# Area attention in a two-layer vision network: where the fill-in projections stand, half sums ahead of the means, and every odd exponential summed by DMA

## The chip, the cores and the metric

The kernel runs on one core of a Trainium2 chip. The metric is the device time of one execution in microseconds (us); three runs before the change took 2905.74, 2909.25 and 2912.93 us, the median being 2909.25 us.

A core has engines that run side by side, each with its own queue of instructions in program order: TensorE (PE in the profile, with its weight loads as PEld), VectorE (DVE), ScalarE (ACT), GpSimd (POOL) and SyncE (SP, which only issues transfers here). An instruction starts when the ones before it in its own queue have started and the semaphores it names have been raised by others. Sixteen DMA engines move data; a DMA that adds into its destination is issued from POOL's queue here.

## The reference, cut to what matters

The network has four parts (attention, a recurrent layer, convolutions with a state-space scan, experts). Only the first one changes:

```python
def _ln_c(v, eps=1e-6):                       # over the 256 channels
    m = jnp.mean(v, axis=1, keepdims=True)
    s = jnp.var(v, axis=1, keepdims=True)
    return (v - m) / jnp.sqrt(s + eps)

x = x + _L0_conv_ref(_ln_c(x), ...)           # x: (2, 256, 64, 64)

# inside _L0_conv_ref: 8 heads of 32 channels, areas of 1024 pixels (16 rows)
qk = _conv1x1_bn(x, w_qk, ...);  vv = _conv1x1_bn(x, w_v, ...)
pp = _bn(conv 5x5, depthwise, of vv)
attn = softmax(einsum('bhdn,bhdm->bhnm', q, k) * hd ** -0.5)
o = einsum('bhdm,bhnm->bhdn', v, attn)
return _conv1x1_bn(o + pp, w_proj, ...)
```

Everything is float32. There are 2 images of 4 areas each, so 8 areas of 1024 tokens, and in each area 8 heads.

## The kernel before

`area_attention` holds the image in SBUF as two channel halves of 128 partitions (`x[:, c]`). An area has two *groups*, one for each channel half `c` (four heads each), so there are 16 groups; `G` numbers the groups and `A` the areas. A group is 16 *steps*: `t = 8 n + m`, where `n` is the half of the queries (512 columns) and `m` a block of 128 keys. The loop over `g` from 0 to 255 writes out the order of all queues by hand; nothing is moved by a scheduler.

One step issues, in this order:

- `scores` (L366 to L385): four bfloat16 matmuls L371 (each row's maximum, in three parts, from `mxs`) and four float32 matmuls L376 into two PSUM tiles of two banks (`wide`, three buffers); ACT takes the exponentials of both, L383, into `sx` (for `m % 4 == 0`) or `ex` (two buffers of each).
- `values` of the step before (L389 into `av_o`).
- `maxima` of the *next* group (L276, again two `wide` tiles): in even steps ACT keeps their positive part (L288), in odd steps DVE finishes them with four reductions (L292). Four tiles a step pass through three buffers, so the second half of the next step's scores needs the buffer of this step's first maxima tile.
- the sums of the softmax, in fours: `total` is the `sx` pair of `m % 4 == 0`; half 0 of every later exponential is added to it by an accumulating DMA from POOL's queue (L591); half 1 by a POOL addition in odd `m` (L593, held back by a hand-made dependency until the DVE reductions begin) and by a DVE addition where `m % 4 == 2` (L600). Two steps after its last addition, `sums` multiplies the total with ones on PE (L389 into `po`), and at every second call DVE turns, inverts and multiplies (L415 to L423).
- taps: 50 DVE operations an area (L335, L346) for the 5x5 convolution, as many a step as the table `TAPS` says.
- the fill-in work of other areas from the tables `MINE`, `SMALL`, `LATE`, `AROUND`, `LATE_AROUND` (with `_FIRST` variants for group 0): projections `query`, `key`, `v_half`, `output` (L166, four passes on PE for 512 columns), `v_tokens` (transposes L239), `mean` and `variance` (L178: both channel halves times a constant matrix), `place` (L316 and small transfers). All of it shares one PSUM bank, `po`. The entries named "around" hold offsets in areas, the others in groups.

An area's norm runs through these steps of the even group (`c = 0`) for the next area: `centre` (DVE L187), `square` (ACT L190), `variance` (PE L178, ACT L179), `root` (DVE transpose L199, POOL L202 and L203, DVE L206), `scale` (DVE L212). `mean` of the area after that stands in the odd group.

The last group has no maxima to prepare, and the one before it no projections of a next area. After the last step, DVE adds the taps and PE projects the last area (L621).

Of the kernel before, what the change touches and what calls it, by code (L numbers as in the profile page):

```python
# [14 lines left out]
ALU = mybir.AluOpType  # L15
# [78 lines left out]
def area_attention(tc, sh, ap):  # L94
# [13 lines left out]
    with ExitStack() as ctx:  # L108
# [30 lines left out]

        minus_half = cp.tile([P, 1], F32, name="minus_half")  # L140
        nc.gpsimd.memset(minus_half, -0.5)
        latest = [None]

        def mark(op):

            latest[0] = op.ins

        def wide():
            return ps1.tile([P, 2, 512], F32, name="ps", tag="ps")

# [19 lines left out]
        def area(A):  # L170
            b, a = AREAS[A]
            return x[:, :, b, a * NA : (a + 1) * NA]

        def average(src, to, half):

            ps = bank()
            for c in range(2):
                nc.tensor.matmul(ps, sh.mean_w, src[c][:, HALVES[half]], start=c == 0, stop=c == 1)  # L178
            nc.scalar.copy(to[:, HALVES[half]], ps)  # L179

        def mean(A, half):
            average([area(A)[:, c] for c in range(2)], temp("pm", A), half)

        def centre(A, c, at=FULL):
            if A not in xns:
                xns[A] = p1.tile([P, 2, NA], F32, name="xn")
            mark(nc.vector.tensor_tensor(xns[A][:, c, at], area(A)[:, c, at], temp("pm", A)[:, at], ALU.subtract))  # L187

        def square(A, c, at=FULL):
            nc.scalar.activation(temp(f"sq{c}", A)[:, at], xns[A][:, c, at], AF.Square)  # L190
# [4 lines left out]
        def root(A, part, at=FULL):  # L195
            n = (at.stop - at.start) // 32
            if part == 0:
                turned = temp("ln_t", A)[:, at]
                mark(nc.vector.transpose(turned, temp("var", A)[:, at]))  # L199
                t = turned.rearrange("p (k i) -> p k i", i=32)[:, :, 0]  # L200
                y = held["root", at.start] = p1.tile([P, NA // 32], F32, name="root")[:, :n]
                nc.gpsimd.tensor_scalar(y, t, 1e-6, None, ALU.add)  # L202
                nc.gpsimd.tensor_tensor(y, y, minus_half.to_broadcast([P, n]), ALU.pow)  # L203
            else:
                y = held.pop(("root", at.start))
                mark(nc.vector.transpose(  # L206
                    temp("ln_r", A)[:, at].rearrange("p (k i) -> p k i", i=32),
                    y.unsqueeze(2).to_broadcast([P, n, 32]),
                ))

        def scale(A, c, at=FULL):
            mark(nc.vector.tensor_tensor(xns[A][:, c, at], xns[A][:, c, at], temp("ln_r", A)[:, at], ALU.mult))  # L212

        def columns(t):
            return lambda k: t[:, k]
# [112 lines left out]
        def taps(A):  # L328

            vh, a = vhs[A], AREAS[A][1]  # L330
            for lower in range(2):
                for c in range(2):
                    if not lower:
                        acc = accs[A, c] = p1.tile([P, AROWS, WW], F32, name=f"acc{c}")
                        nc.vector.tensor_scalar(  # L335
                            acc, vh[:, c, 2 : 2 + AROWS], w_pe[:, c, 12:13], t_pe[:, c : c + 1], ALU.mult, ALU.add
                        )
                        yield
                    for k in range(25):
                        dy, dx = k // 5 - 2, k % 5 - 2  # L340
                        if dy == 0 and dx == 0 or (dy > 0) != lower:
                            continue
                        r0, r1 = window(dy, AROWS, AROWS * a, HH)
                        w0, w1 = window(dx, WW)
                        part = accs[A, c][:, r0:r1, w0:w1]
                        mark(nc.vector.scalar_tensor_tensor(  # L346
                            part, vh[:, c, 2 + r0 + dy : 2 + r1 + dy, w0 + dx : w1 + dx],
                            w_pe[:, c, k : k + 1], part, ALU.mult, ALU.add,
                        ))
                        yield  # L350

        def add_taps(A, c):
            y = ys[A, c]
            mark(nc.vector.tensor_tensor(y, y, accs.pop((A, c)).rearrange("p r w -> p (r w)"), ALU.add))

        def output(A, co, half):
            ps, to = bank(), area(A)[:, co, HALVES[half]]
            project(w["wpr"], co, lambda k: ys[A, k], half, ps)
            mark(nc.vector.scalar_tensor_tensor(to, ps, s_pr[:, co : co + 1], to, ALU.mult, ALU.add))

        def shift(A, co):

# [41 lines left out]
        def sums(G, n, half, exs):  # L404
# [15 lines left out]
            nc.vector.transpose(  # L420
                total.rearrange("p (k i) -> p k i", i=32), small.unsqueeze(2).to_broadcast([P, 512 // 32, 32])
            )
            mark(nc.vector.tensor_tensor(y, y, total, ALU.mult))  # L423

        with ExitStack() as own:
# [58 lines left out]
            maxima(0, 7)  # L486
            join(0, 0, nc.vector)
            place(0, 0)
            v_tokens(0, 0, 1)
            query(0, 1)  # L490

            w_pe = cp.tile([P, 2, 25], F32, name="w_pe")
            for c in range(2):
# [5 lines left out]

        MINE = {0: [(1, query, 1)], 11: [(2, query, 0)], 12: [(2, key, 0)], 15: [(2, key, 1)]}
        SMALL = {2: [(0, place, 1)], 10: [(1, place, 0)]}
        LATE = {7: [(1, join, 0)], 15: [(2, key_difference), (1, join, 1)]}
        AROUND = [
            {
                1: [(-1, shift, 0)], 2: [(0, v_tokens, 1, 0)], 3: [(0, v_tokens, 1, 1)], 4: [(1, variance, 0)],
                5: [(-1, shift, 1)], 6: [(1, variance, 1)], 7: [(-1, output, 0, 0)], 8: [(-1, output, 0, 1)],
                10: [(-1, output, 1, 0)], 14: [(1, v_half, 0, 0)],
            },  # L510
            {
                2: [(1, v_half, 1, 0)], 3: [(1, v_half, 0, 1)], 4: [(1, v_half, 1, 1)],
                6: [(-1, output, 1, 1)], 7: [(1, v_tokens, 0, 0)], 8: [(1, v_tokens, 0, 1)],
                10: [(2, mean, 0)], 14: [(2, mean, 1)],
            },
        ]
        LATE_AROUND = [
            {
                0: [(1, centre, 0)], 1: [(1, square, 0)], 2: [(1, centre, 1), (-1, add_taps, 1)],
                3: [(1, square, 1)], 6: [(1, root, 0)],  # L520
                8: [(1, root, 1), (1, scale, 0)], 10: [(1, scale, 1)],
            },
            {15: [(0, add_taps, 0)]},
        ]

        FIRST = {
            0: [(1, key, 1)], 1: [(1, query, 1)], 11: [(2, query, 0)], 12: [(2, key, 0)], 15: [(2, key, 1)],
        }
        SMALL_FIRST = {5: [(0, place, 1)], 10: [(1, place, 0)]}
        LATE_FIRST = {  # L530
            0: [(1, key_difference)], 3: [(0, join, 1)], 7: [(1, join, 0)], 15: [(2, key_difference), (1, join, 1)],
        }
        LATE_AROUND_FIRST = {
            1: [(1, centre, 0)], 2: [(1, centre, 1), (1, square, 0)], 3: [(1, square, 1)],
            6: [(1, root, 0)], 8: [(1, root, 1), (1, scale, 0)], 9: [(1, scale, 1)],
        }


        AHEAD = {t: [(1, t)] for t in range(16)}
# [2 lines left out]
        for t in range(16):  # L542
            AHEAD_FIRST[t] = [order.pop(0) for _ in range(2 if t < 8 else 1)]

        TAPS = [
            [1, 0, 0, 2, 2, 2, 2, 1, 0, 0, 1, 2, 2, 2, 3, 2],
            [2, 0, 2, 2, 3, 2, 2, 1, 1, 0, 3, 2, 3, 2, 2, 1],
        ]
        TAPS_FIRST = [
            [0] * 10 + [1, 2, 3, 2, 3, 2],  # L550
            [2, 0, 2, 2, 3, 3, 3, 2, 2, 0, 3, 3, 3, 3, 3, 3],
        ]

        def works(G, t, *tables):
# [7 lines left out]
                    f(at, *a)  # L562

        pending, due, total = None, {}, None
        at_end = mybir.DependencyInfo(mybir.DependencyClass.Sync, mybir.DependencyReason.DATA)
        conv = iter(())
        for g in range(16 * len(GROUPS)):
            G, t = divmod(g, 16)
# [10 lines left out]
            exs = scores(G, n, m)  # L579
            if pending is not None:  # L580
                values(*pending)
            works(G, t, SMALL_FIRST if new else SMALL, {})

            mm, before = None, latest[0]
            for k, at in (AHEAD_FIRST if new else AHEAD).get(t, ()):
                if G + k < len(GROUPS):
                    mm = maxima(G + k, at)
            if m % 4 == 0:
                total = exs
            else:  # L590
                nc.gpsimd.dma_start(total[0], exs[0], accum_op=ALU.add)  # L591
            if m % 2:
                add = nc.gpsimd.tensor_tensor(total[1], total[1], exs[1], ALU.add)  # L593
                if mm is not None:
                    tc.add_manual_dep(add.ins, mm.name, at_end, reason="beside the reductions")
                    tc.add_manual_dep(add.ins, before.name, at_end, reason="beside the reductions")
            for _ in range((TAPS_FIRST if A == 0 else TAPS)[c][t]):
                next(conv, None)
            if m % 4 == 2:
                mark(nc.vector.tensor_tensor(total[1], total[1], exs[1], ALU.add))  # L600
            works(G, t, FIRST if new else MINE, AROUND[c])
            if g in due:
                sums(*due.pop(g))
            works(G, t, LATE_FIRST if new else LATE, LATE_AROUND_FIRST if new else LATE_AROUND[c])
            pending = G, n, m, exs
            if m % 4 == 3:
                due[g + 2] = G, n, m // 4, total

        values(*pending)
        last = len(AREAS) - 1  # L610
# [1712 lines left out]
```

## Time and profile before

| what | us |
|---|---|
| median of three runs | 2909.25 |
| the profiled execution, and its span | 2907.71, 2905.9 |
| first step of group 0 starts at | 62.2 |
| groups 0 and 1 | 96.7 and 86.8 |
| groups 2 to 12, from 245.8 to 1157.4 | 82.9 each in the mean (82.2 to 84.4) |
| groups 13 and 14 | 81.5 and 76.6 |
| group 15 and the last projection, 1315.5 to 1402.6 | 87.1 |

The starts of the steps are read off the timeline of PE: a step begins with the first of the four matmuls L371. The steps repeat from group to group almost to the hundredth: in group 4 (from 412.6) they take 5.39, 4.43, 4.40, 4.61, 6.08, 4.43, 5.68, 5.40, 5.35, 4.43, 5.73, 5.40, 5.35, 4.43, 5.68 and 5.40 us. What comes after 1402.6 us (half of the span) isn't touched by the change.

### The profile page before, as it was taken

Reading aid. Unit: us, or ns where it says so; the run is one execution under the profiler, and the core shown is the slowest. Engines: PE = TensorE matmul, PEld = TensorE weight load, DVE = VectorE, ACT = ScalarE, POOL = GpSimd, SP = SyncE. Lnnn points to the kernel's source line nnn. Section 1 sums busy time; section 2 is a strip of 40 time slices with the busy share of each in tenths; the row PEclk is TensorE's granted clock in tenths of the full one; section 3 lists DMA queues with packets and bytes.
Section 4 is the critical chain, followed back from the end, with each engine's and each line's share of the span. In section 5 each row is a group of like instructions: output and inputs, shape, how many; then the busy total and the mean of one; then the engine's idle time right before and its main releaser. Section 6 shows DMA issues by size and latency. Waiting matters only on the chain.

```text
span 2905.9 us, 45896 instructions
## 1 busy us (share of the span) xinstructions
PE 2650.5 (91%) x17286; PEld 1490.6 (51%) x17286; DVE 1991.1 (69%) x3765; ACT 1562.2 (54%) x2641; POOL 1289.3 (44%) x1115
## 2 busy tenths in 40 slices
PE   7999999999999999998799999968886599999994
PEld 2223333333333333222599999933343488888873
DVE  4789888888888888879566666788897622222116
ACT  3667676676767676665244555567645522222223
POOL 1454545444554545445213000058772166666651
PEclk9999999999999999998799999989998799999995
DMA  3333443434343434445231000035552366666658
GB/s 131 66 73 74 80 81 73 81 74 81 75 79 74 80 73 81 78 79 100 80 126 65 1 1 2 1 86 150 143 149 94 113 216 232 220 229 229 221 177 348
DMA packets 86393, 321.04 MB, mean 110 GB/s; under 512 B 17608, under 2 KB 18512, under 8 KB 76432
## 3 DMA queue, kind: packets, MB, share of 16 engines
q0 software_dynamic: 53056, 225.88, 30.5%
q1 hardware_dynamic: 31872, 87.86, 9.4%
q10 hardware_dynamic: 1232, 4.25, 0.4%
q8 instruction: 139, 2.28, 0.3%
q14 instruction: 94, 0.77, 0.1%
HBM read 173.30 MB, written 43.58 MB: 75 GB/s over the span
## 4 chain that ended last, share of the span: by engine, by line
PE 74%; DVE 10%; issue 5%; DMA 4%; POOL 4%; ACT 3%; SPq 0%; DVEq 0%; POOLq 0%; ACTq 0%
PE ps L276 9%; PE ph L2069 9%; PE py L2079 8%; PE av_o L389 7%; PE z L796 7%; PE po L166 7%; PE z L808 7%; PE ps L376 6%; PE ps L371 3%; DMA sx<-ex 2%; DVE hs L1541 2%; PE yp L1551 2%; PE po L178 2%; PE po L389 2%; PE px L2057 1%
## 5 line engine op out<-in xcount | busy, mean ns | idle before, releaser
L346 DVE SCALAR_TENSOR_TENSOR acc<-vh,w_pe,acc 128x1008 f32<-128x1008 f32 (+7 forms) x384 | 534.0, 1393 | 9.5
L383 ACT ACTIVATE ex<-ps 128x1024 f32<-128x1024 f32 x384 | 372.8, 1024 | 177.2 <-PE ps L376 101.9
L591 POOL DMA_DIRECT2D sx<-ex x192 | 167.9, 875 | 594.6 <-ACT ex L383 273.5
L292 DVE CUSTOM_DVE_ANT_0 more<-ps,more 128x512 f32<-128x512 f32 x480 | 303.0, 687 | 154.6 <-PE ps L276 146.0
L2071 ACT ACTIVATE act<-ph,wt 128x256 f32<-128x256 f32 x272 | 128.8, 474 | 386.1 <-PE ph L2069 381.9
L593 POOL TENSOR_TENSOR sx<-sx,ex 128x1024 f32<-128x1024 f32 x128 | 324.5, 2535 | 12.3 <-PE ps L276 6.9
L2059 DVE COPY xt<-px 128x512 f32<-128x512 f32 x68 | 47.1, 692 | 396.7 <-PE px L2057 396.7
L2069 PE MATMUL ph<-xt,wt 128*128 128x256 f32 x1088 | 291.7, 391 | 4.7 <-ACT act L2071 3.0
L376 PE MATMUL ps<-q,k 32*128 32x512 f32 x2048 | 290.9, 607 | 0.0
L2079 PE MATMUL py<-wt,act 128*128 128x256 f32 x1088 | 278.8, 379 | 0.0
L288 ACT ACTIVATE more<-ps 128x1024 f32<-128x1024 f32 x240 | 233.1, 1025 | 30.3 <-ACT rows L320 7.8
L2069 PEld LDWEIGHTS ph<-xt,wt 128*128 128x128 f32 x1088 | 190.7, 191 | 67.0 <-DVE xt L2059 23.5
L796 PE MATMUL z<-xs,u 128*128 128x128 f32 x1872 | 224.5, 277 | 0.0
L796 PEld LDWEIGHTS z<-xs,u 128*128 128x128 f32 x1872 | 218.2, 194 | 0.2 <-issue 0.2
L2079 PEld LDWEIGHTS py<-wt,act 128*128 128x128 f32 x1088 | 202.0, 190 | 24.5
L820 ACT ACTIVATE t<-z,bias 128x128 f32<-128x128 f32 x468 | 136.3, 362 | 145.6 <-PE z L808 145.4
L389 PE MATMUL av_o<-ex,vt 128*32 128x512 f32 x1536 | 208.7, 613 | 0.2 <-ACT ex L383 0.2
L2094 POOL DMA_INDIRECT results<-y,ri x136 | 138.0, 1015 | 138.4 <-DVE y L2087 116.4
L276 PE MATMUL ps<-k,q 32*128 32x512 f32 x1088 | 186.5, 640 | 1.4 <-DVE nm L282 0.7
L808 PE MATMUL z<-xs,v 128*128 128x128 f32 x1512 | 180.1, 276 | 0.1
L808 PEld LDWEIGHTS z<-xs,v 128*128 128x128 f32 x1512 | 174.3, 192 | 0.7 <-DVE xs L827 0.7
L1548 POOL TENSOR_TENSOR cs<-hs,cs 128x1024 f32<-128x1024 f32 x63 | 148.9, 2365 | 54.4 <-DVE hs L1541 33.5
(431 smaller groups left out, 4535.8 us busy)
## 6 DMA issues: line engine op xcount, KB each, us to landing
sx<-ex POOLq DMA_DIRECT2D x192, 512.0 KB, 4.6
cs<-c_rows SPq DMA_DIRECT2D x128, 256.0 KB
y<-results SPq DMA_DIRECT2D x32, 512.0 KB
x<-xrows SPq DMA_DIRECT2D x8, 1024.0 KB
rows<-xt SPq DMA_DIRECT2D x16, 512.0 KB
out_x<-res POOLq DMA_DIRECT2D x15, 512.0 KB, 7.0
xrows<-xn SPq DMA_DIRECT2D x24, 256.0 KB
x<-in_x SPq DMA_DIRECT2D x4, 1024.0 KB
```

What stands on the lines that cost most here:

```text
L276: mm = nc.tensor.matmul(tiles[h // 2][:, h % 2], qs[G, i // HM][head(h), i % HM * P : (i % HM + 1) * P], keys[head(h)], start=True, stop=T ...
L288: nc.scalar.activation(held["more"][j], tiles[j], AF.Relu)
L292: nc.vector.tensor_tensor_reduce(more, tiles[h // 2][:, h % 2], more, -1.0, 3.0e38, ALU.add, ALU.min, accum_out=nms[G][:, 0, h, i : i + 1],)
L346: mark(nc.vector.scalar_tensor_tensor(part, vh[:, c, 2 + r0 + dy : 2 + r1 + dy, w0 + dx : w1 + dx], w_pe[:, c, k : k + 1], part, ALU.mult, ...
L376: nc.tensor.matmul(tiles[h // 2][:, h % 2], k[head(h), m % HM * P : (m % HM + 1) * P], qs[G, n][head(h)], start=False, stop=True, tile_pos ...
L383: nc.scalar.activation(exs[i], tiles[i], AF.Exp, scale=HD**-0.5)
L389: nc.tensor.matmul(to[head(h)], lhs, exs[h // 2][:, h % 2], start=first, stop=last, tile_position=(0, HD * h))
L593: add = nc.gpsimd.tensor_tensor(total[1], total[1], exs[1], ALU.add)
L796: nc.tensor.matmul(z[c][:, g, :m], u[:, k, c, g], xt[:, k], start=g == GATES[0] and k == 0, stop=False, skip_group_check=True,)
L808: nc.tensor.matmul(z[c][:, g, :m], v[:, k, c, g], h[:, k], start=False, stop=k == 1, skip_group_check=True,)
L2069: nc.tensor.matmul(ph[:, hc], wt[:, at : at + P], xt[:, c], start=c == 0, stop=c == 1)
L2079: nc.tensor.matmul(py[:, j], act[:, hc, j * P : j * P + P], wt[:, at : at + C], start=hc == 0, stop=hc == NH - 1,)
```

## The change

The step's order becomes a `BEFORE` table (ahead of the maxima), the maxima, the transfers, and then, in even steps, taps, the `BEHIND` tables, `sums`, the `LATE` tables; in odd steps `BEHIND`, `sums`, taps, `LATE`. In the tables the full projections stand in odd steps (apart from step 0 and the two halves of the variance in step 4), and the sums and most transposes in even ones. `sums` comes three steps after its total instead of two. The POOL additions go, and so do the hand-made dependencies: in odd `m`, half 1 is added by a second accumulating DMA. The DVE addition moves from `m % 4 == 2` behind the maxima to `m % 4 == 3` ahead of them. Two DVE additions an area are new (`mean_sum`, `square_sum`), and the mean and the variance multiply their result alone. One batch of transposes moves from the prologue into step 1.

```diff
-            for c in range(2):
-                nc.tensor.matmul(ps, sh.mean_w, src[c][:, HALVES[half]], start=c == 0, stop=c == 1)
+            for c in range(len(src)):
+                nc.tensor.matmul(
+                    ps, sh.mean_w, src[c][:, HALVES[half]], start=c == 0, stop=c == len(src) - 1
+                )
...
+        def mean_sum(A):
+            nc.vector.tensor_tensor(temp("pm", A), area(A)[:, 0], area(A)[:, 1], ALU.add)
+        def mean_of_sum(A, half):
+            average([temp("pm", A)], temp("pm", A), half)
+        def square_sum(A):
+            nc.vector.tensor_tensor(temp("sq0", A), temp("sq0", A), temp("sq1", A), ALU.add)
+        def variance_of_sum(A, half):
+            average([temp("sq0", A)], temp("var", A), half)
...
-            v_tokens(0, 0, 1)
             query(0, 1)
...
+        BEFORE = [
+            {0: [(1, query, 1)], 3: [(0, place, 1)], 11: [(1, place, 0)]},
+            {3: [(0, place, 1)], 11: [(1, place, 0)]},
+        ]
+        BEFORE_AREA = [{4: [(1, variance_of_sum, 0)]}, {0: [(1, v_half, 0, 0)]}]
+        BEHIND = [
+            {11: [(2, query, 0)], 13: [(2, key, 0)], 15: [(2, key, 1)]},
+            {5: [(1, query, 1)], 9: [(2, query, 0)], 13: [(2, key, 0)], 15: [(2, key, 1)]},
+        ]
+        BEHIND_AREA = [
             {
+                1: [(0, v_tokens, 0, 1), (-1, shift, 0)], 3: [(0, v_tokens, 1, 0)], 4: [(1, variance_of_sum, 1)],
+                5: [(-1, output, 0, 0), (-1, shift, 1)], 7: [(-1, output, 0, 1)], 9: [(-1, output, 1, 0)],
+                12: [(0, v_tokens, 1, 1)],
             },
             {
+                1: [(1, v_half, 1, 0)], 3: [(1, v_half, 0, 1)], 4: [(2, mean_of_sum, 0)],
+                7: [(-1, output, 1, 1)], 8: [(2, mean_of_sum, 1)], 11: [(1, v_half, 1, 1)],
+                12: [(1, v_tokens, 0, 0)],
             },
         ]
+        LATE = {7: [(1, join, 0)], 15: [(2, key_difference), (1, join, 1)]}
+        LATE_AREA = [
             {
+                0: [(1, centre, 0)], 1: [(1, centre, 1), (1, square, 0)], 2: [(1, square, 1)],
+                3: [(-1, add_taps, 1), (1, square_sum)], 5: [(1, root, 0)], 7: [(1, root, 1), (1, scale, 0)],
+                8: [(1, scale, 1)],
             },
+            {3: [(2, mean_sum)], 15: [(0, add_taps, 0)]},
         ]
...
         TAPS = [
-            [1, 0, 0, 2, 2, 2, 2, 1, 0, 0, 1, 2, 2, 2, 3, 2],
-            [2, 0, 2, 2, 3, 2, 2, 1, 1, 0, 3, 2, 3, 2, 2, 1],
+            [2, 0, 0, 1, 2, 2, 1, 1, 0, 1, 0, 3, 2, 2, 2, 3],
+            [2, 1, 1, 2, 2, 2, 2, 2, 2, 1, 1, 3, 2, 2, 2, 1],
         ]
         TAPS_FIRST = [
-            [0] * 10 + [1, 2, 3, 2, 3, 2],
-            [2, 0, 2, 2, 3, 3, 3, 2, 2, 0, 3, 3, 3, 3, 3, 3],
+            [0, 0, 0, 0, 1, 1, 1, 1, 1, 1, 2, 2, 3, 2, 3, 2],
+            [2, 1, 2, 2, 2, 2, 2, 2, 2, 1, 2, 2, 2, 2, 2, 2],
         ]
...
+            if m % 4 == 3:
+                nc.vector.tensor_tensor(total[1], total[1], pending[3][1], ALU.add)
             for k, at in (AHEAD_FIRST if new else AHEAD).get(t, ()):
...
-            else:
-                nc.gpsimd.dma_start(total[0], exs[0], accum_op=ALU.add)
-            if m % 2:
-                add = nc.gpsimd.tensor_tensor(total[1], total[1], exs[1], ALU.add)
-                if mm is not None:
-                    tc.add_manual_dep(add.ins, mm.name, at_end, reason="beside the reductions")
-                    tc.add_manual_dep(add.ins, before.name, at_end, reason="beside the reductions")
-            for _ in range((TAPS_FIRST if A == 0 else TAPS)[c][t]):
-                next(conv, None)
-            if m % 4 == 2:
-                mark(nc.vector.tensor_tensor(total[1], total[1], exs[1], ALU.add))
+            for i in ((), (0, 1), (0,), (0, 1))[m % 4]:
+                nc.gpsimd.dma_start(total[i], exs[i], accum_op=ALU.add)
...
-                due[g + 2] = G, n, m // 4, total
+                due[g + 3] = G, n, m // 4, total
```

An entry such as `4: [(1, variance_of_sum, 0)]` means: in step 4, half 0 of the variance of the next area; the first of the two tables of a pair is for even groups (`c = 0`), the second for odd ones.

## The prediction

> **What bounds the kernel now.** First the page: who is busy where.
>
> ```profile
> PE 2650.5 (91%) x17286; PEld 1490.6 (51%) x17286; DVE 1991.1 (69%) x3765; ACT 1562.2 (54%) x2641; POOL 1289.3 (44%) x1115
> ...
> PE   7999999999999999998799999968886599999994
> ...
> DVE  4789888888888888879566666788897622222116
> ```
>
> The attention is the first 19 or so of 40 slices (to 1402.6 us). There PE is at 9 and DVE at 8: PE sets the pace and DVE has little to spare. By stretches of one group each (columns: length, then busy time of PE, PEld, DVE, ACT, POOL; clock; DMA share):
>
> ```profile
> 412.60:494.80 82.20, 81.29 (x535) 25.42 (x538) 71.87 (x111) 58.68 (x67) 44.01 (x34) 1.00 0.41 78
> ...
> 1315.50:1402.60 87.10, 64.45 (x394) 16.98 (x389) 71.94 (x68) 33.87 (x38) 38.83 (x29) 0.82 0.42 79
> ```
>
> Group 4 shows PE busy for 81.3 of 82.2 us and DVE for 71.9, at full clock. The last group is different: PE is idle for 23 us. Now PE's timeline, steps 5 and 6 of group 4:
>
> ```profile
> 437.49 0.39 PE L371 MATMUL ps<-mx,ones_b 3*128 3x512 bf16 x4
> 437.71 1.03 PE L376 MATMUL ps<-q,k 32*128 32x512 f32 x8
> 438.67 1.06 PE L389 MATMUL av_o<-sx,vt 128*32 128x512 f32 x8
> 439.67 1.32 PE L276 MATMUL ps<-k,q 32*128 32x512 f32 x8
> 440.92 1.06 PE L389 MATMUL po<-sx,ones 128*32 128x512 f32 x8
> 441.92 0.79 PE L371 MATMUL ps<-mx,ones_b 3*128 3x512 bf16 x4
> 442.32 1.24 PE L376 MATMUL ps<-q,k 32*128 32x512 f32 x8
> ...
> 445.68 1.98 PE L178 MATMUL po<-sq,mean_w 128*128 128x512 f32 x4
> 447.60 0.40 PE L371 MATMUL ps<-mx,ones_b 3*128 3x512 bf16 x4
> ```
>
> Differences of starts price a step: 0.22 + 0.96 + 1.00 + 1.25 = 3.43 us bare; the sums add 1.00, a projection 1.92 (445.68 to 447.60), half of that 0.96, a batch of transposes 0.58, `place` 0.16. A step with sums is 4.43, with a projection 5.35. The step behind the sums has L371 0.79 and L376 1.24 for 0.39 and 1.03: its second half waited for a buffer, and 5.68 us passed instead of 5.35. So a short filler in an odd step isn't free: DVE's reductions (starting 0.03 after the maxima, 0.61 each) release the buffer at 3.46 + 1.22 = 4.7 us into the step.
>
> **The change in PE's queue.** A pair of groups holds 32 bare steps (109.8), 20 projections (38.4; 16 true ones and the four of mean and variance, which cost as much), 8 sums (8.0), 4 batches (2.3) and 4 places (0.6): 159.1 of 2 x 82.9 = 165.7 us. Multiplying a sum instead of two halves makes those four 0.96 each and saves 3.8 us. The rest of what could be won is the 6.6 us of waits.
>
> By step, behind the change: an odd step with a projection 5.35 (the buffer at 4.7 is early enough). An even step with sums: ACT's L288 pair starts when the maxima end, 3.45, its first takes 1.02, so the buffer comes at 4.5: 4.5 whatever the short filler. Step 8 also has the copy of `av_o` (0.59, pitch 0.5) ahead of it, so about 4.8. Steps 3 and 11 with `place` 5.5. Step 0, which took 5.4 to 7.2 us because the maxima waited for POOL's `kd`, now has a projection ahead of them: 5.35. The odd group: seven projections 37.5, two with place 11.0, five short steps 22.5, step 8 4.8, step 4 4.5: 80.3. The even group from step 5 to step 0 of the next: 6 x 5.35 + 5.5 + 4 x 4.5 + 4.8 = 60.4; its steps 1 to 4 come below.
>
> **The two new DVE additions**, 1.24 us each (row of L600, 128x1024, mean 1239 ns), lie beside PE, but each has a reader on PE's in-order queue. What is ahead of `square_sum` on DVE is seen in steps 3 and 4 of group 4 (`add_taps`, and the reductions that wait for PE):
>
> ```profile
> 429.25 1.22 DVE L354 TENSOR_TENSOR y<-y,acc 128x1024 f32<-128x1024 f32 x1
> 430.89 0.69 DVE L292 CUSTOM_DVE_ANT_0 more<-ps,more 128x512 f32<-128x512 f32 x1 [0.42 <-PE ps L276]
> ```
>
> Counted from the start of step 1: step 1 holds only transposes, 4.8 by the reductions' buffer; in step 2 ACT still has `shift` and `square` to do (1.15 and 1.06), its exponentials come 0.7 late, and PE's sums end at 9.7. DVE's five sums operations take 3.1 (423.88 to 426.98) to 12.8, the addition that now stands ahead of the reductions 1.1 to 13.9, step 3's reductions 2.5 to 16.4, then a tap 1.2, `add_taps` 1.1, `square_sum` 1.2: 20.0. PE has step 4's scores and values behind it at 17.4 and wants the sum, because half of the variance now stands ahead of the maxima: it waits 2.5 us, with the maxima queued behind, and step 4 ends at 20.0 + 0.96 + 1.25 + 0.96 = 23.2. Before, steps 1 to 4 took 437.49 - 417.96 = 19.5. `mean_sum` in the odd group stands behind step 3's reductions (14.1 to 16.6, after three taps, sums and addition) and two taps: 20.1; PE wants it at 18.9: 1.2 late.
>
> **POOL.** 128 additions (2.5 us, 324.5 us busy on the page) become 128 DMA issues of 0.87: POOL is relieved. But `root`'s power stays in the middle of the queue:
>
> ```profile
> 450.95 0.32 POOL L202 TENSOR_SCALAR root<-ln_t 128x32 f32<-128x32 f32 x1 [4.58 <-DVE ln_t L199]
> 451.35 5.46 POOL L203 TENSOR_TENSOR root<-root,minus_half 128x32 f32<-128x32 f32 x1
> 456.77 0.92 POOL L591 DMA_DIRECT2D sx<-ex  x1
> ```
>
> Behind the change it is issued in step 5, ahead of step 6's transfer. DVE reaches the transpose at 10.5 into step 5, so POOL is free at 16.3 and step 6's DMA lands near 21.3, where step 9's exponential wants that buffer at 20.9. The delay runs on to step 11: nothing if the pairs overlap, up to 3 us if they queue; I take 1.5, the middle, since the transfers' engine time (next) is half of each landing.
>
> ```profile
> q0 software_dynamic: 18959, 69.08, 40.6%
> ...
> sx<-ex POOLq DMA_DIRECT2D x132, 512.0 KB, 4.6
> ```
>
> 132 transfers at 40.6% of 900 us are 2.8 us of all engines each. Five instead of three in four steps (19.7 us) is 14 us, 71%. Of a pair, the second lands between 0.87 and 2.8 us behind the first: 8.2 to 10 us after its step began, and the buffer is wanted again two steps later at about 12. Hidden by 2 us; without that cover each microsecond costs one in every four steps. [...] The trace's issues took 850 to 1207 ns with DVE four fifths busy, median 874, so the row prices 128 more at 0.87. [...]
>
> **Sum.** An area: even group 60.4 + 23.2 + 1.5 = 85.1, odd 80.3 + 1.2 = 81.5: 166.6 for 165.7, so +0.9, over 5.5 areas (groups 2 to 12) +5. The stalls give back what halving and pairing win.
>
> Group 1 had 37 taps and 86.8 us; with 30 it falls to about 82.5: -4. Group 0 and the transposes out of the prologue (56.73 to 58.52, less one step): -2. Group 13, without a mean: -1. Group 14: six odd steps lack a projection and cost 4.7 to 4.8 for DVE, +1. Group 15 has no maxima, steps of 2.3 us, and hangs on the chain of sums, here the chain of waits:
>
> ```profile
> 1324.10 4.50 DMA sx<-ex
> 1329.13 4.59 DMA sx<-ex
> 1334.26 4.55 DMA sx<-ex
> ...
> 1365.25 6.78 DVE acc L346
> ```
>
> Four steps there take three landings with POOL additions between (issues at 1324.1, 1337.5, 1354.4, 1367.4: 14.4 a turn), and taps beside the additions are slow (the nine from 1331.45 on: 15.3 us, 1.7 each for 1.27). Without the additions three landings and issues are 12 a turn, four turns save 10; DVE's 28 taps, additions and sums make 50 us of work from 1318 on, which also ends by 1375 for 1387. I take -11 (bounds: -4 if DVE waits for each landing in turn, -14 if it never does). Total 5 - 4 - 2 - 1 + 1 - 11 = -12 against the profiled 2907.7, itself 1.5 under the median: 2909.3 - 12 = **2897**.
>
> **Rivals.** *Stalls covered* (faster): DVE runs ahead far enough that PE finds both sums ready, and POOL's delay costs nothing. For it: DVE has 11 us of idle a group. Against it: the idle lies elsewhere, the five operations ahead of `square_sum` are in one block. 2.5 + 1.2 + 1.5 = 5.2 an area over 5.5: -28, 2869. *Accumulating pairs become the bound* (slower): second transfers landing later than 12 us after their step began hold the exponentials, ACT, then PE's buffers. It decides from 2 us above my bound; at 0.5 us past it each four steps lose 0.5, 56 times: +28, 2925. For it: 71% load, and the power that bunches five issues. Against it: no landing above 6.3 us now. *The ends don't gain* (no change): group 15 is held by DVE's waits, -4 instead of -11, group 1 gains 1: 2907.
>
> **How the numbers follow.** About 0.3% (8.7 us) can be told from no change, so the line for faster is 2900.5. Forecast 2897 (own range 2886 to 2909): 0.40, of it 0.25 faster, 0.15 same. Covered: 0.16, faster. Pairs or longer stalls: 0.34, slower. Ends without gain: 0.10, same. So faster 0.41, same 0.25, slower 0.34. Range 2871 to 2927: it takes in both outer cases at their prices and leaves a tenth on each side.
>
> **What would show it.** Right: L178 in even groups' step 4 waiting some 2.5 us for DVE's new addition, in odd ones about 1; even steps of 4.5 and odd ones of 5.35 elsewhere; DMA share near 0.7 in a group; a last group near 76 us. Wrong: exponentials that wait for DMA in every four steps (the pairs), no wait ahead of the new L178 matmuls (covered), or taps that are as slow as before without POOL's additions.

## The result, and the profile after

The changed kernel takes 2950.56 us (median of four runs, 2948.14 to 2955.48); the kernel before took 2911.09 beside it. The ratio is 1.014, with a 95% interval from 1.012 to 1.0161: 39.5 us slower, where 12 us faster was predicted, and outside the range. In the profiled execution the attention ends at 1439.9 us instead of 1402.6. These 37.3 us are what the change cost. The profiled span (2953.6) grew by 10.4 us more, in the half behind the attention that nobody touched; that half took between 1502.6 and 1513.7 us in the twelve profiles of this study, so below the attention's end is given beside each median.

First the page of the kernel after: busy time of each engine, then PE and DVE by slices.

```profile
PE 2657.5 (90%) x17234; PEld 1494.0 (51%) x17234; DVE 1955.8 (66%) x3778; ACT 1559.0 (53%) x2641; POOL 1105.6 (37%) x1115
...
PE   7999999989999998998799999968887599999984
...
DVE  4788887878778787877566666788887612222116
```

PE has 52 matmuls less, POOL 184 us less, DVE 35 us less: the engines were relieved, and yet the attention got longer. (PE's busy time on the page rose by 7 us: in the attention it fell by 6, from 1282.2 to 1276.0, and in the half that nobody touched it rose by 14.) In the first 19 slices the 7s between DVE's 8s and the first two 8s in PE's row are new gaps. By stretches (length, then busy time of PE, PEld, DVE, ACT, POOL; clock; DMA share; GB/s), an odd group, an even one, and the last group with the last projection:

```profile
330.10:412.90 82.80, 80.22 (x527) 24.92 (x526) 70.61 (x111) 56.19 (x65) 28.61 (x34) 1.00 0.68 128
412.90:503.30 90.40, 81.85 (x527) 25.59 (x528) 68.59 (x113) 58.10 (x67) 31.28 (x32) 0.98 0.62 117
...
1353.40:1439.80 86.40, 67.60 (x393) 17.02 (x388) 60.62 (x68) 34.30 (x38) 23.87 (x29) 0.91 0.71 135
```

Odd groups stayed at 82.8 us. Group 4, an even one, went from 82.2 to 90.4, with PE idle for 8.5 us instead of 0.9; the six even groups take 88.7 to 90.4 now and took 82.2 to 83.9. The last group didn't gain. Groups 2 to 12 took 951.2 us instead of 911.6, so nearly all of the loss in the middle lies in the even groups.

Even groups lose in two places. The first is step 4, here on PE's timeline (start, length, what, and in brackets the idle time before it and what ended it):

```profile
434.67 0.39 PE L379 MATMUL ps<-mx,ones_b 3*128 3x512 bf16 x2 [1.16 <-DVE nm L300]
...
439.44 1.10 PE L172 MATMUL po<-sq,mean_w 128*128 128x512 f32 x2 [2.52 <-DVE sq L187]
440.46 2.09 PE L284 MATMUL ps<-kd,q 32*128 32x512 f32 x8
442.49 1.81 PE L172 MATMUL po<-sq,mean_w 128*128 128x512 f32 x2
```

and on DVE's:

```profile
435.76 1.26 DVE L354 SCALAR_TENSOR_TENSOR acc<-vh,w_pe,acc 128x1008 f32<-128x1008 f32 x1
436.94 1.22 DVE L362 TENSOR_TENSOR y<-y,acc 128x1024 f32<-128x1024 f32 x1
438.08 1.22 DVE L187 TENSOR_TENSOR sq<-sq,sq 128x1024 f32<-128x1024 f32 x1
```

PE waits 2.52 us for `square_sum` (L187), which stands behind a tap and `add_taps`. The work behind the wait is then slow: L284 takes 2.09 us, where it takes 1.14 in the same place of group 6. The granted clock says why. Two windows of the kernel after, from 1 us behind the end of that wait, in group 4 and in group 6:

```profile
440.46:444.23 3.77, 3.77 (x12) 1.02 (x12) 1.30 (x2) 2.18 (x3) 0.00 (x0) 0.55 0.00 0
613.62:617.39 3.77, 3.77 (x27) 1.28 (x30) 1.32 (x2) 3.10 (x5) 0.00 (x0) 1.00 0.00 0
```

In the same busy time PE does 12 instructions at 0.55 and 27 at 1.00. Group 4 lost half of its clock behind a wait of 2.52 us, group 6 behind the same wait lost nothing (the last section shows where the two waits fell). That is one reason why PE's busy time shrank by so little: by 6.9 us in groups 2 to 12, from 894.4 to 887.5; e1 below, at a clock of 1.00 in group 4, comes to 883.0.

The second place is steps 8 to 12, where POOL's power and the transfers behind it hold the exponentials. POOL's timeline in group 4, then ACT's:

```profile
454.59 1.24 POOL L210 TENSOR_SCALAR root<-ln_t 128x32 f32<-128x32 f32 x1 [5.83 <-DVE ln_t L207]
455.91 6.23 POOL L211 TENSOR_TENSOR root<-root,minus_half 128x32 f32<-128x32 f32 x1
462.11 0.92 POOL L597 DMA_DIRECT2D sx<-ex  x1
467.23 1.76 POOL L597 DMA_DIRECT2D sx<-ex  x2 [4.20 <-DMA sx<-ex]
```

```profile
466.77 1.94 ACT L391 ACTIVATE ex<-ps 128x1024 f32<-128x1024 f32 x2 [1.75 <-DMA sx<-ex]
...
474.68 1.02 ACT L391 ACTIVATE ex<-ps 128x1024 f32<-128x1024 f32 x1 [1.48 <-DMA sx<-ex]
```

The power is ready at 462.1; before, it was at 456.8, in a group that had started 0.3 us earlier. The transfer of step 6 goes out right behind it and lands at 466.7; ACT has waited for that buffer since 465.0, and the queue of transfers passes the delay on to step 11.

Last, the transfers between 400 and 1300 us (share of 16 engines; issues and the median time to landing):

```profile
q0 software_dynamic: 30160, 109.85, 64.8%
...
sx<-ex POOLq DMA_DIRECT2D x210, 512.0 KB, 5.4
```

The share is near the 71% that were worked out; a transfer lands in 5.4 us where it took 4.6, the slowest in 9.9 for 6.3.

### The profile page after: what moved, and what is told of

Its sections match the earlier page's. It is cut to its first block, busy times and chain, and to the rows that moved or that the text cites. A ratio compares the mean times of both kernels' runs of the same rounds, so it can differ in the third digit from the quotient of the medians.

```text
span 2953.6 us, 45858 instructions
## 1 busy us (share of the span) xinstructions
PE 2657.5 (90%) x17234; PEld 1494.0 (51%) x17234; DVE 1955.8 (66%) x3778; ACT 1559.0 (53%) x2641; POOL 1105.6 (37%) x1115
## 4 chain that ended last, share of the span: by engine, by line
PE 68%; DVE 12%; DMA 6%; issue 6%; POOL 4%; ACT 3%; SPq 0%; DVEq 0%; POOLq 0%; ACTq 0%
PE ph L2073 9%; PE ps L284 8%; PE py L2083 8%; PE z L800 7%; PE z L812 7%; PE po L160 6%; PE av_o L397 6%; PE ps L384 5%; DMA sx<-ex 5%; PE ps L379 2%; DVE hs L1545 2%; PE yp L1555 2%; DVE more L300 2%; PE po L397 2%; POOL root L211 1%
## 5 line engine op out<-in xcount | busy, mean ns | idle before, releaser
L597 POOL DMA_DIRECT2D sx<-ex x320 | 280.0, 964 | 814.7 <-ACT ex L391 250.6
L354 DVE SCALAR_TENSOR_TENSOR acc<-vh,w_pe,acc 128x1008 f32<-128x1008 f32 (+7 forms) x384 | 484.0, 1261 | 8.9
L284 PE MATMUL ps<-k,q 32*128 32x512 f32 x1088 | 186.0, 639 | 4.7 <-ACT ex L391 2.5
L379 PE MATMUL ps<-mx,ones_b 3*128 3x512 bf16 x1024 | 137.9, 386 | 52.5 <-ACT more L296 29.5
L391 ACT ACTIVATE sx<-ps 128x1024 f32<-128x1024 f32 x128 | 124.0, 1021 | 94.2 <-PE ps L384 70.3
```

The lines of the kernel that those rows point to most:

```text
L284: mm = nc.tensor.matmul(tiles[h // 2][:, h % 2], qs[G, i // HM][head(h), i % HM * P : (i % HM + 1) * P], keys[head(h)], start=True, stop=T ...
L354: nc.vector.scalar_tensor_tensor(part, vh[:, c, 2 + r0 + dy : 2 + r1 + dy, w0 + dx : w1 + dx], w_pe[:, c, k : k + 1], part, ALU.mult, ALU.add,
L391: nc.scalar.activation(exs[i], tiles[i], AF.Exp, scale=HD**-0.5)
L597: nc.gpsimd.dma_start(total[i], exs[i], accum_op=ALU.add)
```

## The experiments

Four take the change apart (e1 to e4), two put half of it into the kernel before (e6, e7), and four build on what was learned (e5, e8, e9, e10). Each ratio is to runs of the kernel before that were taken beside it. The first step of the attention starts between 59.3 and 65.7 us in these profiles, which shifts the ends too.

| kernel | median us | ratio to before, 95% interval | attention ends at |
|---|---|---|---|
| before | 2909 to 2911 | | 1402.6 |
| after | 2950.6 | 1.014 (1.012 to 1.0161) | 1439.9 |
| e1: after, sums early | 2921.6 | 1.0038 (1.0027 to 1.005) | 1415.9 |
| e2: after, root later | 2934.3 | 1.009 (1.0064 to 1.0116) | 1419.6 |
| e3: after, projection behind the maxima in step 0 | 2941.7 | 1.0111 (1.0089 to 1.0133) | 1433.8 |
| e4: after, POOL additions | 2970.7 | 1.02 (1.0178 to 1.0222) | 1472.2 |
| e5: e1, e2 and e3 together | 2895.7 | 0.9958 (0.9942 to 0.9974) | 1384.8 |
| e6: before, with the halving alone | 2935.1 | 1.0097 (1.008 to 1.0114) | 1431.7 |
| e7: before, with the pairs alone | 2938.3 | 1.0114 (1.0096 to 1.0132) | 1427.6 |
| e8: e5, POOL additions in the last group | 2892.0 | 0.9945 (0.9929 to 0.9961) | 1386.1 |
| e9: e8 without the halving | 2915.0 | 1.0017 (1.0008 to 1.0026) | 1404.0 |
| e10: e8, one DVE addition behind the reductions | 2889.8 | 0.9931 (0.9919 to 0.9943) | 1378.5 |

**e1: the two new DVE additions directly behind a step's reductions.**

```diff
-                1: [...], 3: [(0, v_tokens, 1, 0)], 4: [(1, variance_of_sum, 1)],
+                1: [...], 3: [(0, v_tokens, 1, 0), (1, square_sum)], 4: [(1, variance_of_sum, 1)],
...
-                3: [(-1, add_taps, 1), (1, square_sum)], ...
-            {3: [(2, mean_sum)], 15: [(0, add_taps, 0)]},
+                3: [(-1, add_taps, 1)], ...
+            {15: [(0, add_taps, 0)]},
...
-                1: [(1, v_half, 1, 0)], ...
+                1: [(1, v_half, 1, 0), (2, mean_sum)], ...
```

> The changed kernel with its two new DVE additions moved forward in DVE's queue: square_sum directly behind step 3's reductions (ahead of a tap and add_taps), mean_sum two steps earlier. Theory (PE waits for these sums, 2.5 us in seven areas and 22 us in all for the mean, and the stall also lowers the granted clock in some areas): the waits of L172 for DVE fall from 37 us to under 10, and the time by 20 to 30 us, to 0.45 to 0.8 of the loss of 39.5. Rival (the pairs of accumulating DMAs set the pace, and PE only waits there because it is early): the time falls by less than 8 us, and exponentials wait longer for DMA later on.

Measured: 29.0 us below the kernel after (2950.6 - 2921.6). Step 4 of the even groups fell from 10.25 us in the mean to 7.16, that of the odd ones (groups 3 to 11) from 6.22 to 4.72. PE's timeline in group 4 of e1:

```profile
437.31 1.10 PE L172 MATMUL po<-sq,mean_w 128*128 128x512 f32 x2 [0.21 <-DVE sq L187]
438.34 1.14 PE L284 MATMUL ps<-kd,q 32*128 32x512 f32 x8
```

The wait is 0.21 us (1.2 us in the six even groups together), and L284 behind it takes 1.14 us; the clock from 412 to 503 us is 1.00. So the place of two DVE additions, which cost no engine anything, was worth three quarters of the loss.

**e2: POOL's power one step later, behind the transfer.**

```diff
-                3: [...], 5: [(1, root, 0)], 7: [(1, root, 1), (1, scale, 0)],
-                8: [(1, scale, 1)],
+                3: [...], 6: [(1, root, 0)], 8: [(1, root, 1), (1, scale, 0)],
+                9: [(1, scale, 1)],
```

> The changed kernel with root and scale one step later, so that step 6's transfer is issued ahead of POOL's 7.5 us of root. Theory (the transfer that is late behind root holds steps 9 to 11 of the even groups, 28.0 us for steps 8 to 12 where 24.7 were worked out): steps 8 to 12 fall to about 25, seven areas gain 20 to 25 us. Rival (a pair lands too late by itself, 5.3 us median and up to 9.9): steps 8 to 12 stay within 1 us of 28.0, gain under 6.

Measured: 16.3 us in the median, 20.3 in the attention. Steps 8 to 12 of the even groups went from 28.0 to 24.1 us, where 24.65 had been worked out for a POOL that is never late. Waits of ACT between groups 2 and 12, of the kernel after:

```profile
ACT ex L391 <- DMA sx<-ex: 25.1, 16, 2.7
```

and of e2:

```profile
ACT ex L391 <- DMA sx<-ex: 0.4, 1, 0.4
```

These waits, 25.1 us in 16 of them, were the power's and not the pairs': the pairs are the same in both kernels.

**e3: in step 0 the projection behind the maxima again.**

```diff
-            {0: [(1, query, 1)], 3: [(0, place, 1)], 11: [(1, place, 0)]},
+            {3: [(0, place, 1)], 11: [(1, place, 0)]},
...
-        BEFORE_AREA = [{4: [(1, variance_of_sum, 0)]}, {0: [(1, v_half, 0, 0)]}]
+        BEFORE_AREA = [{4: [(1, variance_of_sum, 0)]}, {}]
```

Both entries go to step 0 of `BEHIND` and `BEHIND_AREA` (in group 0, `key` and `query` both stand there).

> The changed kernel with step 0's projection behind the maxima again. Theory (ahead of the maxima it hides kd but no longer covers the release of the buffer that step 1 waits for; steps 0 and 1 of odd groups take 11.6 us, 10.7 were worked out): steps 0 and 1 fall by 0.9 in each of 15 groups, 10 to 14 us in all. Rival (the wait for kd comes back, 0.5 to 0.7 us a group): within 5 us of the changed kernel.

Measured: 8.9 us in the median, 6.1 in the attention, less than expected. Steps 0 and 1 together went from 11.63 to 11.27 us in odd groups. In the kernel after, step 0 was short (5.06), but step 1 took 6.57. With the projection ahead of them, the maxima are the last work of step 0, and PE wants their first buffer back at once; ACT gives it back 2.3 us after they start. PE's timeline there, in group 5, and ACT's:

```profile
507.39 1.14 PE L284 MATMUL ps<-kd,q 32*128 32x512 f32 x8
...
509.69 0.39 PE L379 MATMUL ps<-mx,ones_b 3*128 3x512 bf16 x2 [0.95 <-ACT more L296]
```

```profile
508.62 1.94 ACT L296 ACTIVATE more<-ps 128x1024 f32<-128x1024 f32 x2 [0.28 <-PE ps L284]
```

In e3 the wait for POOL's `kd` is back (step 0 takes 5.9), and step 1 is 5.35.

**e4: POOL additions instead of the second transfers, all else as after.**

```diff
-            for i in ((), (0, 1), (0,), (0, 1))[m % 4]:
-                nc.gpsimd.dma_start(total[i], exs[i], accum_op=ALU.add)
+            if m % 4:
+                nc.gpsimd.dma_start(total[0], exs[0], accum_op=ALU.add)
+            if m % 2:
+                nc.gpsimd.tensor_tensor(total[1], total[1], exs[1], ALU.add)
```

> The changed kernel with half 1 of odd exponentials added by POOL again (2.5 us each) instead of a second DMA, without the old hand-made dependency. If pairs of DMAs are what was lost: landings fall from 5.3 to 4.6 us, group 15 shrinks by 8 to 12 us, the whole by 15 to 25. If not (order of the queues is what was lost): POOL's additions lie beside DVE's taps, which take twice as long there, root's block grows by two additions, and the time is 0 to 20 us above the changed kernel.

Measured: 20.1 us slower than the kernel after. Step 14 of the even groups takes 9.9 us instead of 4.5. DVE's timeline of e4 there, and PE's behind it:

```profile
489.11 10.64 DVE L354 SCALAR_TENSOR_TENSOR acc<-vh,w_pe,acc 128x992 f32<-128x992 f32 x5
```

```profile
501.02 0.39 PE L379 MATMUL ps<-mx,ones_b 3*128 3x512 bf16 x2 [2.83 <-DVE nm L300]
```

Five taps beside two POOL additions take 2.1 us each, where the mean of a tap in the kernel after is 1.27; DVE's reductions come late, and PE waits 2.83 us for them. So the second transfers were not what the change lost by: in this order of steps they are worth 20 us.

**e6: the halving alone, in the kernel before** (`mean_sum` behind the sums of step 9, `square_sum` behind the taps of step 3, one product each):

```diff
-                3: [(1, square, 1)], 6: [(1, root, 0)],
+                3: [(1, square, 1), (1, square_sum)], 6: [(1, root, 0)],
...
-            {15: [(0, add_taps, 0)]},
+            {9: [(2, mean_sum)], 15: [(0, add_taps, 0)]},
```

> The kernel before, with only the channel halves added ahead of the means and variances (mean_sum in step 9 of odd groups, square_sum behind the squares of step 3), all tables else as before. Theory (PE saves 0.96 us in each of 26 half multiplications, 0.85 where a buffer then binds, and DVE has room for 2.5 us an area there): 12 to 22 us under the kernel before. Rival (DVE, four fifths busy, is late with them): no gain, or slower.

Measured: 25.9 us slower, where 12 to 22 faster were expected. The mistake of the prediction was made again. PE's timeline of e6 in step 4 of group 4, and in step 10 of group 5:

```profile
446.18 2.08 PE L178 MATMUL po<-sq,mean_w 128*128 128x512 f32 x2 [2.37 <-DVE sq L193]
448.19 0.61 PE L385 MATMUL ps<-mx,ones_b 3*128 3x512 bf16 x4
448.59 1.92 PE L390 MATMUL ps<-q,k 32*128 32x512 f32 x8
...
564.07 1.10 PE L178 MATMUL po<-pm,mean_w 128*128 128x512 f32 x2 [2.07 <-ACT more L302]
565.10 0.47 PE L385 MATMUL ps<-mx,ones_b 3*128 3x512 bf16 x4
565.35 1.93 PE L390 MATMUL ps<-q,k 32*128 32x512 f32 x8
```

and DVE's in the latter:

```profile
562.10 0.69 DVE L437 TENSOR_TENSOR y<-y,sum 128x512 f32<-128x512 f32 x1
562.71 1.22 DVE L187 TENSOR_TENSOR pm<-x 128x1024 f32<-128x1024 f32 x1
```

The trace puts the second wait down to ACT's L302, which ended at 564.02. But in the kernel before L178 starts in this step ahead of that same operation (548.78, L288 at 548.93). What is new for it is DVE's `pm`, done at 563.93 behind the operations of the sums; L178 starts at 564.07. Behind both of these waits the matmuls take 1.92 us for 1.24. A window of e6 over the six microseconds behind the first has this clock (the third number from the end):

```profile
446.00:452.00 6.00, 5.82 (x22) 1.36 (x22) 2.59 (x3) 2.03 (x3) 0.00 (x0) 0.50 0.00 0
```

**e7: the pairs alone, in the kernel before** (the sums two steps behind their total, as they were):

```diff
-                add = nc.gpsimd.tensor_tensor(total[1], total[1], exs[1], ALU.add)
+                nc.gpsimd.dma_start(total[1], exs[1], accum_op=ALU.add)
```

(the two hand-made dependencies on `add` go with it).

> The kernel before, with only POOL's additions replaced by second accumulating DMAs. Theory (the pairs by themselves are hidden in groups 1 to 14): steady groups keep 82 to 83 us, group 15 changes by 5 us at most, the whole within 8 us of before. Rival (pairs are the bound): landings of 5.3 us and more hold the exponentials, steady groups grow by over 1 us each, 15 us or more in all.

Measured: 29.1 us slower, where nothing beyond 8 was expected. Odd groups didn't change. Even ones did, in two steps; PE's timeline of step 9 and DVE's of step 3 show it:

```profile
466.59 1.05 PE L389 MATMUL po<-sx,ones 128*32 128x512 f32 x4 [1.59 <-DMA sx<-ex]
```

```profile
427.97 1.22 DVE L597 TENSOR_TENSOR sx<-sx,ex 128x1024 f32<-128x1024 f32 x1 [1.65 <-DMA sx<-ex]
```

In step 9 the sums wait on PE for the pair of step 7. In the odd groups two steps are enough for a pair, and no sums wait there for a landing. In the even ones this pair stands behind the power on POOL:

```profile
453.76 5.46 POOL L203 TENSOR_TENSOR root<-root,minus_half 128x32 f32<-128x32 f32 x1
...
459.80 1.22 POOL L593 DMA_DIRECT2D sx<-ex  x1
```

In step 3 the DVE addition, which came late enough for a POOL addition, now waits for a transfer, with the reductions behind it, for which PE waits 1.69 us in step 4. The last group with its projection grew too, from 87.1 to 92.4 us. The kernel after has a third step of delay and the DVE addition a step later; which of the two the pairs need isn't shown, since no run has only one of them.

**e5: e1, e2 and e3 together.**

> The three edits of the first experiments together: the sums earlier in DVE's queue, root one step later, step 0's projection behind the maxima. Theory (three separate losses in the order of the queues): they add, 29 + 16 + 9 us below the changed kernel, so 2890 to 2903, under the kernel before (2911). Rival (one bound behind all three, the DMA pairs): the gains overlap and the time stays at 2910 or more.

Measured: 2895.7 us, below both kernels. 2950.6 - 29.0 - 16.3 - 8.9 = 2896.4: the three losses were apart from one another. Even groups take 82.2 us, odd ones 81.0.

**e8: e5, and in the last group alone POOL additions.**

```diff
+            by_pool = G == len(GROUPS) - 1
             for i in ((), (0, 1), (0,), (0, 1))[m % 4]:
+                if i and by_pool:
+                    nc.gpsimd.tensor_tensor(total[1], total[1], exs[1], ALU.add)
+                else:
+                    nc.gpsimd.dma_start(total[i], exs[i], accum_op=ALU.add)
-                nc.gpsimd.dma_start(total[i], exs[i], accum_op=ALU.add)
```

> The three edits together, and in the last group alone POOL's additions again in place of second DMAs. Theory (the last group hangs on its chain of landings, which pairs make longer: steps 0 to 15 took 60.8 us with pairs and 56.0 with POOL's additions): 3 to 6 us under the kernel with the three edits. Rival (DVE's taps set its end, slowed by POOL's additions): no gain, or some us lost.

Measured: 3.7 us below e5 in the median, where the intervals overlap, so that a gain isn't shown. The last group's sixteen steps start within 56.3 us instead of 60.2, but what follows the last of them takes 30.9 us instead of 25.2: the group with its projection went from 85.5 to 87.2 us. The rival's reason shows in the taps there, in e5 and then, beside POOL additions, in e8:

```profile
1349.57 6.13 DVE L354 SCALAR_TENSOR_TENSOR acc<-vh,w_pe,acc 128x930 f32<-128x930 f32 x5
```

```profile
1349.04 10.11 DVE L354 SCALAR_TENSOR_TENSOR acc<-vh,w_pe,acc 128x930 f32<-128x930 f32 x5
```

Over all runs neither way wins: the last group and the projection take 85.2 to 86.5 us with pairs (after, e1, e2, e3, e5) and 83.7 to 87.7 with POOL additions (e4, e8, e9, e10). The chain of waits of the kernel after (start, length, what) shows what a pair costs there:

```profile
1366.37 5.98 DMA sx<-ex
...
1373.68 6.52 DMA sx<-ex
...
1393.41 6.45 DMA sx<-ex
...
1407.24 8.08 DMA sx<-ex
...
1415.85 6.11 DMA sx<-ex
```

**e9: e8 without the halving** (two products per half again, no additions):

```diff
-            average([temp("pm", A)], temp("pm", A), half)
+            average([area(A)[:, c] for c in range(2)], temp("pm", A), half)
...
-            average([temp("sq0", A)], temp("var", A), half)
+            average([temp(f"sq{c}", A) for c in range(2)], temp("var", A), half)
```

(and `mean_sum`, `square_sum` go from the tables).

> The kernel of e8 (2892.0 us), but mean and variance are again two products each (both halves of the channels multiplied and added up in PSUM), without the two DVE additions; all else, the steps they stand in too, stays. Theory (the halving is worth its PE time once its additions stand early): four products of 0.96 us come back for each of six and a half pairs of groups, in steps where PE is the bound; step 4 and the short odd steps take part of it into their waits: even groups 82.2 to about 83.5, odd groups 81.0 to about 82.5, in all 14 to 22 us above e8. Rival (what PE saves goes into DVE's two additions of 1.22 us, which the reductions behind them have to wait for): within 4 us of e8.

Measured: 23.0 us above e8 in the median, 17.9 in the attention. Step 4 of the even groups takes 8.62 us for 7.15, steps 4 and 8 of the odd ones 5.57 and 5.35 for 4.71 and 4.49 (group 5). Groups 2 to 12 take 914.5 us for 898.6: 15.9, or 2.9 for each of 5.5 areas, of the 3.8 that the PE time alone gives. The halving, which cost 26 us in e6, wins 23 here.

**e10: the DVE addition of step 3 (L590) and its pair behind the reductions and `square_sum`, in even groups.**

```diff
+            behind = t == 3 and c == 0
-            if m % 4 == 3:
+            if m % 4 == 3 and not behind:
                 nc.vector.tensor_tensor(total[1], total[1], pending[3][1], ALU.add)
...
+            if behind:
+                works(G, t, BEHIND_FIRST if new else BEHIND[c], BEHIND_AREA[c])
+                nc.vector.tensor_tensor(total[1], total[1], pending[3][1], ALU.add)
             for i in ((), (0, 1), (0,), (0, 1))[m % 4]:
```

> The kernel of e8, but in step 3 of each even group the DVE addition of the third exponential (1.22 us, ahead of the reductions) and the pair of DMAs behind it go behind the reductions and square_sum. In e8 the second half of the maxima behind step 3 waits 1.16 us for those reductions (nm), which start at 424.97, when that addition ends. Theory: the wait of 1.16 goes, step 3 and 4 together get 1.0 shorter, even groups 82.2 to about 81.2: 5 to 8 us below e8 over eight such steps. Rival: the sums on DVE (five operations that end at 423.8) or square_sum, which then comes at the same time as before for a PE that is earlier, take the place of it: no change within 2 us; or the pair that lands 3.5 us later holds up an exponential: slower.

Measured: 7.6 us earlier at the end of the attention, and 2.3 in the median, where the intervals overlap with e8's. Step 4 of the even groups takes 6.41 us for 7.15, and groups 2 to 12 take 894.4 for 898.6, so some 4 are the edit's. Beside it the first step started 2.6 us earlier, the last group, whose code is the same, took 3.5 less, and groups 0 and 14 took 2.7 more: that 7.6 lies in the expected range is in part luck. How much is left over whole runs isn't settled. Two windows of e10, an odd and an even group, stand against those of the kernel after:

```profile
322.30:403.40 81.10, 80.17 (x531) 25.00 (x534) 70.76 (x111) 55.98 (x65) 28.45 (x34) 1.00 0.69 131
403.40:484.80 81.40, 78.42 (x527) 24.65 (x526) 68.11 (x111) 57.78 (x67) 30.59 (x32) 1.00 0.69 130
```

The even group has the same work as in the kernel after and is 9 us shorter, 5.6 of them idle PE.

## Why the prediction was wrong

**The sign came from the stalls.** The prediction's own working gives 6 x 85.1 + 5 x 81.5 = 918.1 us for groups 2 to 12; 951.2 were measured, 33.1 more. That is two thirds of the error (12 + 37.3 = 49.3 us in the attention). Of the three stalls below it had listed the first two, each at the right instruction, and priced them too low; the third it had put at nothing. Over the eleven groups they cost 13, 11 and 5 us more than the sum had for them:

- *Step 4 of the even groups.* "It waits 2.5 us" was right to 0.02. But the wait began later: PE's sums ended 11.0 us into step 1 (429.00 - 417.96), not 9.7, since step 1 took 5.24 us, not 4.8, and step 2 was longer too; the whole chain moved by 1.3. And the price of a wait was taken to be its length. The clock that fell behind it in three groups of six added 1.5 to 1.6 us each time, by where the wait fell on the clock's raster. Steps 1 to 4 took 25.4 us for 23.2. e1 took the wait away and won 29 us.
- *The power.* "Nothing if the pairs overlap, up to 3 us if they queue; I take 1.5, the middle" failed: steps 8 to 12 took 28.0 for 24.65, so 3.4. The transfers queue, and POOL itself was slower: 1.24 and 6.23 us for 0.32 and 5.46. A bound whose upper end is what the profile's own sequence gives should not have been halved. e2 showed that the power's place was the cause.
- *Step 0.* "Now has a projection ahead of them: 5.35" was right for step 0 (5.06), but step 1 paid, with the wait of 0.95 us for ACT's buffer: 11.63 for 10.7 in odd groups. The prediction had this buffer in its sum for the short steps ("4.5 whatever the short filler") and left it out where the maxima come last behind a projection.

**Odd groups** were otherwise near what was worked out: 4.48 in the short steps (4.5) and 5.40 with projections (5.35). Step 4 took 6.22 (4.5 + 1.2), which makes 3 us over the five groups; PE waited 1.44 there. Group 1 took 82.0 (82.5), the DMA share was 0.68 (0.7), an issue on POOL took 0.87 as priced, and group 13 got 0.3 us shorter (1). Groups 0 and 14 came 2.4 and 2 us worse.

**The last group**: "three landings and issues are 12 a turn" failed. It was taken from landings of 4.5 us, each alone; in pairs they are 6 to 8, and a turn of four steps took 16 to 18 us (the issues of its steps 3, 7, 11 and 15 are at 1372.9, 1388.7, 1405.4 and 1423.8). The taps did become fast, ten microseconds for eight, and then waited for landings. The group took 86.4 us for 76: 10 us, a fifth of the error. Where POOL adds again, it is no shorter (e8).

**The gains were real.** Halving was worth 2.9 us an area, of 3.8, once nothing waited for it (e9); the pairs were worth 20 us in this order of steps (e4). The rival *accumulating pairs become the bound*, which stood for "slower", was wrong: with the power out of the way, ACT waited 0.4 us for landings in eleven groups (e2), with as many transfers. The slower outcome came for the most part from the forecast's own stalls at a higher price. Its chance for "pairs or longer stalls" names them, but no rival priced them longer; the only one for them had them at zero.

## What to carry to other kernels

When an operation on PE's path is fed by a new addition on another engine, place the addition by what is queued ahead of it there, not by when its data is ready: the place of the same two additions, and nothing else, was worth 29 us (e1). Price a wait on a full PE at more than its length (in the kernel after, behind three of six waits of 2.4 to 2.5 us, the lower clock added 1.5 to 1.6 us), and take a bound's upper end where the queue's own sequence gives it. Before a transfer takes over a sum, look at its landing time, at who reads the sum, and at what stands ahead of the transfer in the queue that issues it (e7). Work whose buffer the next step needs at once, as the maxima here, should not come last in its step (e3).

## What the runs showed of the hardware

**Short waits lowered PE's clock, by where they fell.** The granted clock in the traces of the kernel before and of the kernel after is 1.00 or 0.50. Within each of the two the stretches of half clock in the attention stand on one raster of 3.41 us, each one to five raster steps long (3.41 to 17.07 us). Between groups 2 and 12 of the kernel after, PE waited for `square_sum` six times, for 2.52 us each (2.39 in group 8). Behind the waits in groups 4, 8 and 12 half clock follows for 3.41 us; behind those in groups 2, 6 and 10 it doesn't. Behind PE's other waits there, of 1.44 us at most, it never did. Here are steps of the raster around the wait of 2.52 us, two in group 4 and three in group 6:

```profile
437.07:440.48 3.41, 1.04 (x5) 0.31 (x5) 3.41 (x3) 0.72 (x1) 0.00 (x0) 1.00 0.92 175
440.48:443.90 3.42, 3.42 (x11) 1.00 (x10) 1.28 (x2) 1.85 (x3) 0.00 (x0) 0.50 0.00 0
...
607.73:611.14 3.41, 2.25 (x18) 0.58 (x17) 3.41 (x8) 1.94 (x2) 0.73 (x1) 1.00 0.94 175
611.14:614.56 3.42, 1.93 (x10) 0.61 (x10) 3.38 (x4) 0.59 (x1) 0.00 (x0) 1.00 0.71 135
614.56:617.97 3.41, 3.41 (x26) 0.97 (x22) 0.42 (x1) 3.09 (x4) 0.00 (x0) 1.00 0.00 0
```

In group 4 PE is idle for 2.37 us of one raster step, and the next one runs at half clock. In group 6 the wait is split between two, with 1.16 and 1.49 us of idle PE, and the clock stays at 1.00. The other four go the same way: PE is idle for 2.39 and 2.52 us of one raster step in groups 8 and 12, and for at most 1.47 and 1.27 in groups 2 and 10. The kernel before has no half clock between groups 2 and 12; the longest idle time in one raster step there is 1.75 us, in a wait of 1.99 us for POOL's `kd` in group 9. In e6 the clock was 0.50 behind the wait of 2.37 us (446.00 to 452.00), and in e7 L376 took 1.88 us behind the wait of 1.69 us in step 4 (at 432.74) and 1.03 in step 5. From what idle time on the clock falls isn't shown.

**Accumulating transfers of 512 KB landed later in pairs**: in the kernel before they took at least 4.5 us and 4.6 in the median, in the kernel after 5.3 in the median and up to 9.9. **POOL beside DVE**: a tap of 1.27 us took 2.1 beside POOL additions (e4).
